# A graph-network kernel's eigensolver: which engine scales the product row and copies the turned column, and who orders GpSimd in the merge levels

## The chip, the cores and the metric

One core of one Trainium2 chip. The time is device microseconds for one launch; all times below are in microseconds (us) unless marked ns. Three runs of the kernel before gave 2366.21, 2367.70 and 2367.98, so the median is 2367.7.

## The reference

`x` has 64 graphs of 256 nodes with 256 features, and `adj` is one 256 x 256 matrix, all fp32. Two layers follow each other:

```python
h = max(layernorm(x), 0)                       # layer 0
x = x + S(S'(S'(h, W1), W2), W3)               # S(h, W) = (adj*adj) @ (h @ W), S' = relu(S)
h = max(layernorm(x), 0)                       # layer 1
deg = A.sum(0) + A.sum(1) - diag(A)            # A = adj
L = rsqrt(deg)[:, None] * (diag(deg) - A) * rsqrt(deg)[None, :]
U = eigh(L).eigenvectors                       # 256 x 256
x = x + U @ (relu((U.T @ h) @ W1' + b1) @ W2' + b2)
```

Layer 0 and the first product of layer 1 (`h @ W1'`) need nothing of the eigenvectors; the rest of layer 1 needs `U`.

## The kernel before

Two kinds of work share the core. The **eigensolver** (class `Eigen`) is one long dependent chain, most of it on VectorE (DVE): it forms L, brings it to tridiagonal form with 254 Householder steps (`tridiagonalize`), solves 16 x 16 leaves (`leaves`), and merges them in four levels of blocks of 32, 64, 128 and 256 (`level`, called from `join`). **Layer 0** (class `Layers`) is TensorE (PE) work on 32 pairs of graphs, with ScalarE (ACT) emptying PSUM banks, GpSimd (POOL) doing the small norm arithmetic and issuing accumulating DMAs. After the eigenvectors are there, layer 1 runs.

**What sets the order.** While the eigensolver is written down, the class `Pace` keeps a model clock for each engine. An eigensolver instruction goes through `Pace.chain`: it works out when its inputs are ready, adds 0.4 on PE or 0.1 on ACT, lets `run` issue layer-0 instructions ("streams") that start before that limit, and then issues its own. A matmul that would pass the limit may be cut at 128 columns (`Op.cut`). The clock uses prices from `Op.__init__`; those of the chain are raised by 6% (`SLOWER = 1.06`). Inside `manual_schedule(engines={PE, Activation})` the program order that results is the order on PE and ACT. The orders on DVE and POOL are left to the framework's scheduler, which works by its own estimate of times. `Pace.fits` decides whether a stream's instruction may go ahead of the limit: with a margin for PE and ACT, and for other engines whenever it starts before the limit.

**A Householder step** on column k (`lo = k + 1`), in the names of the code; a slice `r` has 256 - lo columns, so rows shrink from 255 to 2; up to lo = 127 both halves of 128 rows are live ("first half", 127 steps), afterwards one ("second half", 127 steps):

- `xa`: product of the matrix `a` with the row `xr`, one DVE instruction for each live half, and `ac`, a column.
- `as_row` turns a column into a row: a PE transpose for each live half into PSUM. `pu` (tile psB) is the turned `ac`, `pr` (psA) the turned column `rc = a[:, :, lo]`. The two are issued one after the other, `pu` first.
- scalars: `den`, `gam = 1/den`, `gg = gam*gam`, `gu = gg*u1`, the last two on POOL in the first half and on DVE in the second (`aside`).
- `uau` = sum of `pu * xr`; `gr = pu * gam`, a row, copied out of PSUM with the scale in it; `both = gr*u1 - pr`; `f`; the next row `xn = xr*f - both`; `c`; `wr = xr*c - gr`.
- the update of `a`: two row instructions for each live half, with `wr`, `xr` and the columns `uc`, `wc`.

In the profile a tile has the name of its buffer: `gams` is z, `us` is q, `nbs` is m, `a` is A, the rows r0 and r1 (`junk`, `both`) are r, and `xn` is xr. All kernel lines show as L208, the one place that issues a recorded operation, so the views are read by tile.

**In a level** POOL does three kinds of eigensolver instructions, all `pow` (for `rdq`, `zh`, `rn`). Between them stand layer 0's: three for each norm (`v`, `scale`, `shift`) and three accumulating DMAs for each pair.

Of the kernel before, what the change touches and what calls it, by code (L numbers as in the profile page):

```python
# [23 lines left out]
OP = mybir.AluOpType  # L24
# [14 lines left out]
LEVELS = [32, 64, 128, 256]  # L39
# [120 lines left out]
class Pace:  # L160
# [9 lines left out]
    LEAD = 1.5  # L170

    def __init__(self, nc):
        self.slower, self.lead, self.no_haste = self.SLOWER, 0.0, False
        self.now = Proxy(nc, self.chain)
        self.later = Proxy(nc, lambda op: op)
        self.clock = dict.fromkeys(ENGINES.values(), 0.0)
        self.written, self.read, self.streams, self.on = {}, {}, [], True
# [39 lines left out]
        return self.issue(op, self.slower)  # L217

    def fits(self, op, start, limit, engine):
        if engine is None or op.engine not in ("PE", "ACT"):  # L220
            return start < limit
        if engine == "PE":
            return start < limit + self.HOP * (op.engine == "ACT")
        return start + op.busy + self.lead * (op.engine == "ACT") < limit
# [55 lines left out]
class Eigen:  # L280
# [47 lines left out]
    def row(self, tag):  # L328
        return self.mp.tile([P, N], F32, tag=tag, name=tag)
# [113 lines left out]
    def tridiagonalize(self, a):  # L443
# [6 lines left out]
        nc = self.nc  # L450
# [7 lines left out]
        def as_row(tag, column, halves):  # L458
            ps = self.psum(tag)
            for h in halves:  # L460
                nc.tensor.transpose(
                    ps[:, h * P : (h + 1) * P],
                    column[:, h : h + 1].to_broadcast([P, P]),
                    ident[:, 0, 0:P],
                )
            return ps

        row = lambda tag: self.sp.tile([P, N], F32, tag=tag, name=tag)
# [5 lines left out]
        aside = lambda lo: nc.gpsimd if lo < P else nc.vector  # L474

        def below(xr, lo):

            rest = slice(lo + 1, N)
            sq, tail, alpha = self.row("junk"), *(t[:, lo - 1 : lo] for t in (tails, alphas))
            if lo < P:  # L480
                nc.scalar.activation(sq[:, rest], xr[:, rest], AF.Square, accum_out=tail)
            else:
                self.stt(sq[:, rest], xr[:, rest], 1.0, xr[:, rest], OP.mult, OP.mult, accum=tail)
            nc.gpsimd.tensor_copy(alpha, xr[:, lo : lo + 1])
            return alpha, tail

        def length(xr, lo, tail):

            nn, s0, q, qn = (self.col(c, 1) for c in ("nn", "s0", "q", "qn"))
            x1 = xr[:, lo : lo + 1]  # L490
            self.stt(nn, x1, x1, tail, OP.mult, OP.add)
            if lo < P:
                self.power(s0, nn, 0.5)
                nc.gpsimd.tensor_scalar(q, x1, 0.0, 0.5, OP.is_ge, OP.subtract)
                return nn, s0, q, None
            nc.scalar.activation(s0, nn, AF.Sqrt, bias=guard)
            self.ts(q, x1, 0.0, OP.is_ge, 0.5, OP.subtract)
            self.tt(qn, q, nn, OP.mult)
            return nn, s0, q, qn

        xc = self.col("xc")
        self.tt(xc, a[:, :, 0], self.lower[:, :, 0], OP.mult)
        xr = row("xr")
# [3 lines left out]
        for k in range(N - 2):  # L507
            lo = k + 1
            r, rest = slice(lo, N), slice(lo + 1, N)
            halves = [0, 1] if lo < P else [1]  # L510
            hs = slice(halves[0], H)
            rc = a[:, :, lo]

            nb = nbs[:, k : k + 1]
            if qn is not None:
                rs, qs = self.col("rs", 1), self.col("qs", 1)
                self.recip(rs, s0)
                self.tt(qs, q, s0, OP.mult)
            xa, junk = self.col("xa"), self.row("r0")
            for h in halves:  # L520
                self.stt(junk[:, r], a[:, h, r], 1.0, xr[:, r], OP.mult, OP.mult, accum=xa[:, h : h + 1])
                if h == halves[0] and qn is not None:
                    self.stt(nb, rs, qn, qs, OP.mult, OP.add)
            if qn is None:
                self.stt(nb, q, 2.0, s0, OP.mult, OP.mult)

            ac, uc = self.col("ac"), us[:, :, k]
            self.stt(ac[:, hs], rc[:, hs], nb, xa[:, hs], OP.mult, OP.add)
            pu, pr = as_row("psB", ac, halves), as_row("psA", rc, halves)

            none = self.col("none", 1)
            nc.gpsimd.tensor_scalar(none, tail, 1e-30, 1e30, OP.is_le, OP.mult)
            nc.gpsimd.tensor_tensor(none, none, nn, OP.add)
            den, gg, gu = (self.col(c, 1) for c in ("den", "gg", "gu"))
            gam = gams[:, k : k + 1]
            u1 = xr[:, lo : lo + 1]
            self.tt(u1, u1, nb, OP.add)
            self.stt(den, alpha, nb, none, OP.mult, OP.add)
            self.recip(gam, den)
            self.stt(uc, ident[:, :, lo], nb, xc, OP.mult, OP.add)  # L540
            aside(lo).tensor_tensor(gg, gam, gam, OP.mult)
            aside(lo).tensor_tensor(gu, gg, u1, OP.mult)
            gc, gr = self.col("gc"), row("gr")
            if halves[0]:
                self.tt(gc[:, hs], ac[:, hs], gam, OP.mult)
            else:
                self.ts(gc, ac, gam, OP.mult)

            uau, c = self.col("uau", 1), self.col("c", 1)
            self.stt(junk[:, r], pu[:, r], 1.0, xr[:, r], OP.mult, OP.mult, accum=uau)  # L550
            self.ts(gr[:, r], pu[:, r], gam, OP.mult)

            xn, xcn, both, f = row("xr"), self.col("xc"), self.row("r1"), self.col("f", 1)
            self.stt(both[:, rest], gr[:, rest], u1, pr[:, rest], OP.mult, OP.subtract)
            self.stt(f, uau, gu, gr[:, lo : lo + 1], OP.mult, OP.subtract)
            self.stt(xn[:, rest], xr[:, rest], f, both[:, rest], OP.mult, OP.subtract)
            more = lo + 1 < N - 1
            if more:
                alpha1, tail1 = below(xn, lo + 1)
            self.stt(c, uau, 0.5, gg, OP.mult, OP.mult)  # L560
            wr, wc = row("wr"), self.col("wc")
            self.stt(wr[:, r], xr[:, r], c, gr[:, r], OP.mult, OP.subtract)
            self.stt(wc[:, hs], uc[:, hs], c, gc[:, hs], OP.mult, OP.subtract)
            if more and halves[0]:
                following = length(xn, lo + 1, tail1)
            if halves[0]:
                nc.gpsimd.memset(xcn[:, 0:1], 0.0)
            self.stt(xcn[:, hs], gc[:, hs], u1, rc[:, hs], OP.mult, OP.subtract)
            self.stt(xcn[:, hs], uc[:, hs], f, xcn[:, hs], OP.mult, OP.subtract)
            aside(lo).tensor_tensor(xcn[:, hs], xcn[:, hs], self.lower[:, hs, lo], OP.mult)  # L570
            if more and not halves[0]:
                following = length(xn, lo + 1, tail1)

            for h in halves:
                self.stt(a[:, h, r], wr[:, r], uc[:, h : h + 1], a[:, h, r], OP.mult, OP.add)
                self.stt(a[:, h, r], xr[:, r], wc[:, h : h + 1], a[:, h, r], OP.mult, OP.add)
            xr, xc = xn, xcn
            if more:
                alpha, tail, (nn, s0, q, qn) = alpha1, tail1, following
# [9 lines left out]
        dc = self.col("dnew")  # L589
# [1155 lines left out]
    def join(self, u, ut, bad, reflections=None):  # L1745
        d = self.row("DV")
        self.nc.vector.tensor_copy(d, self.d)
        self.pace.slower, self.pace.lead = self.pace.IN_BLOCKS, self.pace.LEAD
        if reflections is not None:
            reflections = Stream(self.reflections(*reflections))  # L1750
            self.pace.streams = reflections, *self.pace.streams
        zt, dc = self.leaves(d, self.e, bad)
        if reflections is not None:
            self.pace.complete(reflections)
        self.pace.slower, self.pace.lead = self.pace.SLOWER, 0.0
        for n in LEVELS:
            dc = self.level(n, zt, dc, self.rho, self.sg, bad)
        z = self.mat("m0")
        self.copy_out(z, self.transpose(zt))
        self.product(u, self.qt, z)  # L1760
        self.product(ut, z, self.qt)
# [631 lines left out]
```

## Time and profile before

| what | value |
|---|---|
| median of 3 runs | 2367.7 |
| the profiled execution's own time | 2369.36 |
| its span, first to last instruction | 2367.6 |
| TensorE clock granted over the span | 0.994 |
| tridiagonal steps (tile gr) | 25 to 1299 |
| leaves (tile chain from 1324) | to about 1665 |
| levels (matmul psB for zt at 1679, flag at 2173.8) | 1680 to 2173 |
| layer 1 on U (`bank<-hw,u`) | 2181 to 2363 |

The profile has busy times by engine, a picture of 40 slices, groups of instructions by tile, waits (who waited for whom), and a timeline. In a timeline row the first number is the start, the second the duration of the group from its first start to its last end, and what stands in brackets is the engine's idle time before it with the instruction that ended it. Durations on DVE overlap: an instruction that reads 215 ns can be followed by the next start after 120 ns, so the difference of two starts is what an instruction costs its engine. An fp32 matmul of 256 columns is recorded as two instructions.

### The profile page before, as it was taken

The page shows a single profiled execution, that of the slowest core. Times are in us where ns is not written, and L with a number is a line of the kernel's source. Part 1 is how long each engine was busy: PE and PEld are TensorE (multiplying, and loading weights), DVE is VectorE, ACT ScalarE, POOL GpSimd, SP SyncE. Part 2 cuts the span into 40 slices and gives each one's busy share as a digit, 9 for nine tenths or more (in the row PEclk, how much of TensorE's full clock was granted, in tenths as well). Part 3 has the DMA queues.
Part 4 walks back from the last instruction along what each step waited for, and adds up shares of the span by engine and source line. Part 5 has one row for each costly group of instructions (what it writes and reads, how often), then busy time and mean ns, then how long its engine had stood idle before and what let it go on. Part 6 is the DMA issues. An engine that isn't in the chain of part 4 may idle for free. (4 is left out here: it accounts for less than half of the span.)

```text
span 2367.6 us, 40804 instructions
## 1 busy us (share of the span) xinstructions
PE 2290.2 (97%) x10652; PEld 1854.7 (78%) x10652; DVE 2005.0 (85%) x12072; ACT 1183.8 (50%) x2951; POOL 698.7 (30%) x1946
## 2 busy tenths in 40 slices
PE   7999999999999999999999899999999999999999
PEld 4687878787777877787888788777778777887888
DVE  7999999999999999999999899999877687882343
ACT  4455554555555555555555345555554455543322
POOL 3444544445554222222222001111111111111443
PEclk9999999999999999999999999999999999999999
DMA  4022222122222222222222222322322222223675
GB/s 134 23 70 61 65 57 70 51 69 63 59 59 62 72 56 61 69 67 59 72 63 60 58 63 72 72 72 59 72 63 63 59 58 72 54 63 103 217 251 203
DMA packets 91359, 183.26 MB, mean 77 GB/s; under 512 B 8432, under 2 KB 61808, under 8 KB 91120
## 3 DMA queue, kind: packets, MB, share of 16 engines
q0 software_dynamic: 13392, 73.14, 15.6%
q1 hardware_dynamic: 77728, 107.45, 13.4%
q8 instruction: 86, 1.41, 0.2%
q14 instruction: 153, 1.25, 0.2%
HBM read 65.48 MB, written 41.94 MB: 45 GB/s over the span
## 5 line engine op out<-in xcount | busy, mean ns | idle before, releaser
L208 PE MATMUL bank<-forms,L_gnn_W 128*128 128x256 f32 (+2 forms) x2102 | 490.7, 382 | 9.2 <-DVE x L208 6.1
L208 PE MATMUL bank<-L_gnn_W,s 128*128 128x256 f32 x2086 | 476.0, 378 | 4.8 <-ACT s L208 4.7
L208 PEld LDWEIGHTS bank<-forms,L_gnn_W 128*128 128x128 f32 x2102 | 390.6, 191 | 73.3 <-issue 11.7
L208 PEld LDWEIGHTS bank<-L_gnn_W,s 128*128 128x128 f32 x2086 | 391.7, 192 | 57.3 <-ACT s L208 5.7
L208 ACT ACTIVATE s<-bank 128x512 f32<-128x512 f32 (+1 forms) x485 | 278.7, 579 | 174.3 <-PE bank L208 173.3
L208 PE MATMUL bank<-forms,sums 128*128 128x256 f32 (+1 forms) x1512 | 347.0, 377 | 0.0
L208 PEld LDWEIGHTS bank<-forms,sums 128*128 128x128 f32 x1512 | 283.3, 191 | 53.4 <-issue 15.5
L208 PE MATMUL bank<-gt,s 128*128 128x256 f32 (+1 forms) x1036 | 246.3, 377 | 1.1 <-ACT s L208 1.1
L208 PE MATMUL bank<-L_gnn_W,y 128*128 128x512 f32 (+3 forms) x538 | 230.8, 572 | 1.1 <-ACT y L208 1.1
L208 ACT ACTIVATE forms<-bank 128x512 f32<-128x512 f32 x217 | 128.9, 594 | 180.9 <-PE bank L208 180.7
L208 PEld LDWEIGHTS bank<-gt,s 128*128 128x128 f32 x1036 | 188.9, 190 | 24.8 <-ACT s L208 2.6
L208 POOL COPY m<-xr 128x1 f32<-128x1 f32 x254 | 59.9, 236 | 418.1 <-DVE xr L208 418.0
L208 PEld LDWEIGHTS bank<-L_gnn_W,y 128*128 128x128 f32 x538 | 98.7, 190 | 98.2 <-issue 87.3
L208 ACT ACTIVATE junk<-xr 128x254 f32<-128x254 f32 (+63 forms) x127 | 46.0, 362 | 200.5 <-DVE xr L208 200.4
L208 ACT ACTIVATE junk<-x 128x256 f32<-128x256 f32 x256 | 105.8, 413 | 71.9 <-issue 44.0
L208 DVE SCALAR_TENSOR_TENSOR A<-xr,wc,A 128x255 f32<-128x255 f32 (+63 forms) x381 | 139.2, 368 | 0.0
L208 DVE SCALAR_TENSOR_TENSOR A<-wr,q,A 128x255 f32<-128x255 f32 (+63 forms) x381 | 138.0, 365 | 0.0
L208 ACT ACTIVATE junk<-x,nm 128x256 f32<-128x256 f32 x256 | 128.7, 503 | 4.0
L208 PE MATMUL bank<-p,gt 128*128 128x512 f32 (+2 forms) x272 | 122.8, 567 | 0.0
L208 PE MATMUL bank<-gt,h 128*128 128x256 f32 (+1 forms) x520 | 119.1, 379 | 0.1
L208 DVE SCALAR_TENSOR_TENSOR r<-A,xr 128x255 f32<-128x255 f32 (+63 forms) x381 | 117.8, 309 | 0.2
L208 PE MATMUL psB<-ident,ac 128*128 128x128 f32 x381 | 84.7, 277 | 27.2 <-DVE z L208 15.0
(614 smaller groups left out, 4639.5 us busy)
## 6 DMA issues: line engine op xcount, KB each, us to landing
x<-in_x_dram SPq DMA_DIRECT2D x128, 256.0 KB, 3.0
x<-x SPq DMA_DIRECT2D x64, 512.0 KB, 3.5
forms<-forms POOLq DMA_DIRECT2D x31, 768.0 KB, 5.8
s<-s POOLq DMA_DIRECT2D x31, 768.0 KB, 5.9
s<-forms POOLq DMA_DIRECT2D x31, 768.0 KB, 5.8
hw<-hw SPq DMA_DIRECT2D x64, 256.0 KB, 3.1
out_dram<-out SPq DMA_DIRECT2D x64, 256.0 KB, 2.2
L_gnn_W<-in_L_gnn_W_dram SPq DMA_DIRECT2D x1, 2048.0 KB, 11.2
```

The costliest lines, as they stand in the source:

```text
L208: return op.call(*op.args, **op.kwargs)
```

## The change

In the Householder step the scale by `gam` leaves the row and goes to columns and scalars: `gr` is gone, its readers take `pu` out of PSUM; the column `ug = uc*gam` is new, `gu` is now `gam*u1`, `hg = gam*0.5` (POOL in every step) replaces `gg`, and `f` takes two instructions. The transpose of `rc` goes from behind that of `ac` to the start of the step, and ACT copies its result from PSUM into an SBUF row `pr`. In the levels, POOL joins PE and ACT in the program order that `Pace` makes, and a stream's POOL instruction goes ahead of an eigensolver's POOL instruction only if it ends before that one's limit.

```diff
     def fits(self, op, start, limit, engine):
+        if self.pool_too and engine == "POOL" == op.engine:
+            return start + op.busy < limit
         if engine is None or op.engine not in ("PE", "ACT"):
             return start < limit
...
             rc = a[:, :, lo]
+            turned, pr = as_row("psA", rc, halves), row("pr")
+            nc.scalar.copy(pr[:, rest], turned[:, rest])
...
-            pu, pr = as_row("psB", ac, halves), as_row("psA", rc, halves)
+            pu = as_row("psB", ac, halves)
...
-            den, gg, gu = (self.col(c, 1) for c in ("den", "gg", "gu"))
+            den, hg, gu = (self.col(c, 1) for c in ("den", "hg", "gu"))
...
-            aside(lo).tensor_tensor(gg, gam, gam, OP.mult)
-            aside(lo).tensor_tensor(gu, gg, u1, OP.mult)
-            gc, gr = self.col("gc"), row("gr")
+            aside(lo).tensor_tensor(gu, gam, u1, OP.mult)
+            nc.gpsimd.tensor_scalar(hg, gam, 0.5, None, OP.mult)
+            gc, ug = self.col("gc"), self.col("ug")
...
+            self.ts(ug, uc, gam, OP.mult)
...
             self.stt(junk[:, r], pu[:, r], 1.0, xr[:, r], OP.mult, OP.mult, accum=uau)
-            self.ts(gr[:, r], pu[:, r], gam, OP.mult)
...
-            self.stt(both[:, rest], gr[:, rest], u1, pr[:, rest], OP.mult, OP.subtract)
-            self.stt(f, uau, gu, gr[:, lo : lo + 1], OP.mult, OP.subtract)
+            self.stt(both[:, rest], pu[:, rest], gu, pr[:, rest], OP.mult, OP.subtract)
+            self.stt(t, uau, gu, pu[:, lo : lo + 1], OP.mult, OP.subtract)
+            self.tt(f, t, gam, OP.mult)
             self.stt(xn[:, rest], xr[:, rest], f, both[:, rest], OP.mult, OP.subtract)
...
-            self.stt(c, uau, 0.5, gg, OP.mult, OP.mult)
+            self.tt(c, uau, hg, OP.mult)
             wr, wc = row("wr"), self.col("wc")
-            self.stt(wr[:, r], xr[:, r], c, gr[:, r], OP.mult, OP.subtract)
-            self.stt(wc[:, hs], uc[:, hs], c, gc[:, hs], OP.mult, OP.subtract)
+            self.stt(wr[:, r], xr[:, r], c, pu[:, r], OP.mult, OP.subtract)
+            self.stt(wc[:, hs], ug[:, hs], c, gc[:, hs], OP.mult, OP.subtract)
...
-            self.stt(xcn[:, hs], gc[:, hs], u1, rc[:, hs], OP.mult, OP.subtract)
+            self.stt(xcn[:, hs], ac[:, hs], gu, rc[:, hs], OP.mult, OP.subtract)
...
             for h in halves:
-                self.stt(a[:, h, r], wr[:, r], uc[:, h : h + 1], a[:, h, r], OP.mult, OP.add)
+                self.stt(a[:, h, r], wr[:, r], ug[:, h : h + 1], a[:, h, r], OP.mult, OP.add)
...
         self.pace.slower, self.pace.lead = self.pace.SLOWER, 0.0
-        for n in LEVELS:
-            dc = self.level(n, zt, dc, self.rho, self.sg, bad)
+        self.pace.pool_too = True
+        with self.tc.manual_schedule(engines={mybir.EngineType.Pool}):
+            for n in LEVELS:
+                dc = self.level(n, zt, dc, self.rho, self.sg, bad)
+        self.pace.pool_too = False
```

## The prediction

> **What bounds the kernel now.** I read the busy times and the picture first, then the windows by stage, then PE's waits, then the timeline around the long ones.
>
> ```profile
> PE 2290.2 (97%) x10652; PEld 1854.7 (78%) x10652; DVE 2005.0 (85%) x12072; ACT 1183.8 (50%) x2951; POOL 698.7 (30%) x1946
> ...
> PE   7999999999999999999999899999999999999999
> ...
> DVE  7999999999999999999999899999877687882343
> ```
>
> PE is full in nearly every slice, also after the solver ends; DVE, which carries the solver, is full only up to the levels. The same by stage (first the window and its length, then busy PE, PEld, DVE, ACT, POOL):
>
> ```profile
> 56.00:1318.00 1262.00, 1237.64 (x5948) 999.99 (x5947) 1186.03 (x7454) 679.43 (x1745) 495.37 (x1646) 1.00 0.26 62
> 1318.00:1680.00 362.00, 351.52 (x1588) 284.30 (x1587) 336.99 (x2647) 182.90 (x474) 37.36 (x81) 1.00 0.26 63
> 1680.00:2173.00 493.00, 476.03 (x2145) 386.90 (x2145) 371.49 (x1678) 247.27 (x570) 63.91 (x96) 0.98 0.26 63
> 2173.00:2368.00 195.00, 186.48 (x850) 160.70 (x849) 69.03 (x103) 48.50 (x90) 81.10 (x67) 0.98 0.65 222
> ```
>
> PE is idle 24.4 in the tridiagonal steps, 10.5 in the leaves, 17.0 in the levels, 8.5 after the flag. When the solver ends, layer 0 is nearly, not quite, used up: fourth products of the last pair (`L_gnn_W,s`) still run from 2173 to 2185, and its last rows at 2202. So a shorter solver only moves layer-0 matmuls from beside it to behind it. **The time changes by PE's idle time and PE's slow clock, not by DVE's busy time.** PE's waits name the places:
>
> ```profile
> PE psB L208 <- DVE z L208: 15.0, 19, 1.9
> PE psB L208 <- DVE xr L208: 10.6, 12, 1.7
> PE bank L208 <- ACT s L208: 8.6, 6, 3.8
> ...
> PE bank L208 <- DVE x L208: 6.1, 5, 3.6
> PE psA L208 <- DVE m L208: 4.8, 1, 4.8
> ```
>
> The first two are `pu`'s transposes: 26 us in 31 waits over the steps, some 0.8 each. Those steps hold 36 DVE adds of layer 0 (`x<-x,bank`, 0.68 each) that DVE's own order puts among the solver's instructions, as many as there are waits; PE comes to the transpose on time and DVE is late by one add. (z and xr come one to three instructions after `ac`, which is what psB really needs.) The long waits cost twice:
>
> ```profile
> 1763.96 1.89 PE L208 MATMUL bank<-gt,s 128*128 128x256 f32 x8
> 1769.61 6.55 PE L208 MATMUL bank<-L_gnn_W,s 128*128 128x256 f32 x16 [3.76 <-ACT s L208]
> ...
> 1764.14 0.72 POOL L208 TENSOR_TENSOR rdq<-rdq,half 128x2 f32<-128x2 f32 x1 [4.36 <-DVE rdq L208]
> 1764.94 0.19 POOL L208 TENSOR_SCALAR v<-v 128x4 f32<-128x4 f32 x1
> ...
> 2158.35 3.78 PE L208 MATMUL psA<-q,m 128*128 128x256 f32 x8 [4.82 <-DVE m L208]
> ...
> 2168.43 1.89 PE L208 MATMUL psA<-m,QT 128*128 128x256 f32 x8
> ```
>
> Sixteen such matmuls take 3.62 elsewhere and 6.55 after the wait at 1769; eight take 3.78 against 1.89. The windows of 10 us from 1770, 1880 and 2160 show a granted clock of 0.73, 0.77 and 0.78. A wait of 3.6 to 4.8 so costs about 3 more.
>
> **Part 1, the scale to columns.** By differences of DVE starts near 403 (row of 194) and 1000 (row of 76): `gr` goes (0.33; 0.21), in the second half also `gg` (0.07); `c` becomes a plain product (0.12 to 0.07). `ug` comes: a 128x2 instruction costs 0.12 (`uc`) to 0.29 (`gc`, whose reader follows at once); `f` needs one more, 0.07. A first-half step saves 0.20 to 0.03, a second-half one 0.21 + 0.07 + 0.05 - 0.07 - (0.12 to 0.29), so 0.14 to a loss of 0.03. Over 127 steps of each kind: 43 to 0. I take 30, as `ug` stands among independent instructions, like `uc`. It also stands where DVE waits for psB now (22.3 in 74 waits), so part of that wait is filled. All of it lies beside PE's work: the solver ends about 30 earlier, and that alone is worth 0 to the sum. `gu`, until now needed by `f`, is needed by `both`, one row earlier; POOL does it in 0.20 while `gc`, `ug` and `uau` run, and today's wait for `gg` is 0.2 in all. If layer 0's `pow` of 1.04 stands ahead of it, DVE loses up to 1 us in some of 65 places; beside PE again.
>
> What it does to PE goes through the clock of `Pace`. That charges a scalar product 0.126, where the trace shows 0.07; `gr` out at 0.35, `ug` and the second half of `f` in at 0.13 each, so its first-half step shrinks by 0.08 and the real one by up to 0.20. PE is given about 0.1 more work a step than DVE needs, and a late DVE is caught up in fewer steps. Bounds: the 24 stay, or all go. I take a quarter off: **-6**.
>
> One rule speaks against leaving the product in PSUM. Row first: `both` with a PSUM input takes 347 ns (`r<-gr,xr,psA`), `xn` from SBUF alone 345 (`xr<-xr,f,r`), `wr` 346. The Trainium skill, "VectorE: DVE Perf Modes", section "Rules for kernel authors", advises to copy PSUM to SBUF first where many operations follow, and its table in "The TRN2 errata" gives 120 fixed cycles against 58. By the page `wr`, the one row that newly reads PSUM, would lose an estimated 65 ns a step, 16 us of DVE; by the rows nothing. DVE is not the bound, so neither moves the sum.
>
> **Part 2, `rc` turned at the start, copied by ACT.** 254 ACT instructions come: 0.28 for 128x128 out of PSUM, 0.37 for 128x256, so about 75 us in an engine that is busy 679 of 1262; PE waits for no ACT row in the steps from 56 to 1318, so I cost them at nothing. The copy waits in ACT's queue for the transpose; behind it are bank emptyings, with four banks. Were that cover gone, each copy could hold ACT some 0.3. The two transposes keep their 0.11 each. But each step has a second meeting of PE with DVE (in the first half a third: `rc`'s halves become ready at different times). For 254 meetings the trace shows about 90 cuts: `forms,L_gnn_W` needs 31 pairs x 32 matmuls x 2 = 1984 instructions and has 2102, `sums` 1512 for 1488, `s` 2086 for 2048; that is 59, 12 and 19. Two 128-column pieces cost 0.23 twice against 0.43 whole, 0.03 a cut. With 380 more meetings, 0 to 380 cuts, by the same share 135: **+4**. What waits they add: bounded by a rival below, 0 to 38, taken as 0, since a PE that has just waited at psA is on time at psB.
>
> **Part 3, POOL by the clock.** At 1764 the norm's inputs had been ready since 1762.3; `v` stood behind `rdq`, which DVE released at 1764.1. So `shift` came 2 us late, ACT's four `h` instructions waited 2.65 for it, `s` behind them in ACT's queue, and PE 3.76. With `Pace` placing POOL's instructions that one goes first: 3.8 + 2.9 slow clock, **-7**. But a `pow` of the solver then waits behind a norm's three (1.4) or a DMA issue (0.9) more often, beside PE; and everything after is shuffled: the stage shows four long PE waits in 493 us, two of them layer 0's own (the other, 4.6 on `DVE x` near 1872 plus 3 slow, lies in DVE's order and stays). Half a new one: **+3**. Bounds: -14 (both go) to +14.
>
> **Part 4, what the earlier end does.** At 2153 PE has nothing but the last pair left, which waits for its DMA, so 4.8 idle and 3.2 slow follow; near 2192 the last norm costs 2.8 + 0.5 and 1.1 slow. With 30 us of layer 0 left over, the first has cover and the second partly falls beside layer 1's matmuls: **-8 and -2**. If the solver ends less than about 10 earlier, both stay.
>
> **Sum:** -6 + 4 - 7 + 3 - 8 - 2 = -16 on the profiled 2369.4 (span 2367.6 and 1.8 around it), 2353.4. That execution stands 1.7 above the median, so 2352.
>
> **Rivals.**
> *Much better, 2340:* PE is so late throughout that DVE's late adds never reach it: 18 more of the 24 go, and some in the leaves, -12 in all beyond the forecast. For: DVE already waits for psB in 74 steps. Against: 31 PE waits exist beside them.
> *Nothing moves, 2364:* the program is PE's work, the clocked POOL order gives one wait and makes another, the end keeps its last-pair gaps: only the -6 and +4 of the steps remain, and perhaps a wait saved. For: 2290 of 2368 is matmul. It is also the case in which POOL's order comes out as it was.
> *Slower, 2378:* PE comes too early to `rc`. Near 406, DVE runs `xa` of the first half (0.28) before the last update of `a` (406.39), though the program, and so `Pace`, has them the other way; PE's transposes now come 0.1 to 0.4 after `ac` is ready. A margin of 0.3 is gone, and PE could stand up to 0.3 in each of 127 steps. Price 127 x 0.25 = 32, less 12 of psB's waits that it replaces, and the -6 is lost: 2352 + 26. It decides from 0.13 a step on (16 us). Against: in the second half one half is live and the order is the program's, and PE has the more slack the more `Pace` overcharges.
>
> **Numbers.** Forecast 2352 (2345 to 2361) 0.48; much better 0.14; nothing moves 0.22; slower 0.16. The measurement can tell about 0.2% (4.7 us) from no change. Of "nothing moves" I put 0.05 below 2363, 0.14 within, 0.03 above. Faster 0.48 + 0.14 + 0.05 = 0.67, same 0.14, slower 0.19. The range reaches to 2338 and to 2376, leaving out the far ends of the outer cases, under 0.2.
>
> **What would show it.** Right: tridiagonal steps shorter by some 30, PE's idle there near 20 and now partly at psA, the flag near 2140, no PE wait over 3 in the last 60 us before it, and a clock over 0.994. Wrong: PE's waits for psA in the steps above 25 us; new PE waits for ACT rows there; a `pow` of the solver that PE ends up waiting for in the levels; or a solver that does not end earlier.

## The result, and the profile after

Five runs of the changed kernel gave a median of 2392.1 (2390.3 to 2395.3), five of the kernel before 2367.4 (2364.7 to 2368.0): by the medians it is **24.7 slower**, and the ratio on record is 1.0111 times the time before, interval 1.0100 to 1.0123. The forecast was 2352, its range 2338 to 2376. The profiled execution took 2391.75 with a span of 2390.0. All lines of the changed kernel show as L209.

The head of the page (engine, busy time, share of the span, instructions) and three groups (last columns: busy, mean ns of one, idle time before them and what ended most of it):

```profile
PE 2298.2 (96%) x10936; PEld 1854.1 (78%) x10936; DVE 1966.2 (82%) x12199; ACT 1246.8 (52%) x3205; POOL 725.4 (30%) x2073
...
L209 PE MATMUL psA<-ident,A 128*128 128x128 f32 x381 | 107.4, 283 | 45.1 <-DVE A L209 34.7
...
L209 DVE SCALAR_TENSOR_TENSOR r<-psB,xr 128x255 f32<-128x255 f32 (+63 forms) x254 | 73.4, 289 | 69.5 <-PE psB L209 66.0
L209 ACT COPY pr<-psA 128x254 f32<-128x254 f32 (+63 forms) x254 | 66.7, 263 | 119.6 <-PE psA L209 118.5
```

The same stages by windows (window, length, then busy PE, PEld, DVE, ACT, POOL, granted clock):

```profile
56.00:1318.00 1262.00, 1210.99 (x6014) 971.44 (x6013) 1145.59 (x7560) 711.24 (x1929) 516.02 (x1761) 1.00 0.24 59
1318.00:1680.00 362.00, 347.28 (x1563) 278.81 (x1562) 336.44 (x2652) 184.36 (x478) 39.01 (x83) 1.00 0.27 65
1680.00:2173.00 493.00, 486.67 (x2230) 395.79 (x2229) 373.74 (x1684) 257.48 (x593) 70.10 (x100) 1.00 0.28 72
2173.00:2390.00 217.00, 212.78 (x992) 184.14 (x990) 68.13 (x99) 65.97 (x130) 79.29 (x68) 1.00 0.60 192
```

PE's idle time in the four stretches was 24.4, 10.5, 17.0 and 8.5 and is now 51.0, 14.7, 6.3 and 4.2: 15.8 more in all. Its busy time grew by 8.0. Together that is 23.8, against 22.4 that the span grew (the first 56 us are left out of the idle time). So the loss lies in the tridiagonal steps, 26.6 more idle, and the levels and the end give back 15. DVE's busy time in the steps fell by 40, from 1186.0 to 1145.6, yet the steps end where they did: the leaves begin at 1325.2 (1323.7 before). What DVE saved became waiting, as its waits below show.

PE's and DVE's waits over the whole span (waiting engine and its tile, releaser; us, times, longest):

```profile
PE psA L209 <- DVE A L209: 34.7, 42, 2.7
PE psA L209 <- DVE qs L209: 8.5, 11, 1.4
...
PE bank L209 <- ACT s L209: 4.4, 6, 1.4
PE psB L209 <- DVE z L209: 4.4, 9, 0.9
PE psB L209 <- DVE xr L209: 4.3, 9, 1.4
```

```profile
DVE r L209 <- PE psB L209: 66.0, 141, 2.7
```

At psB PE waits 8.7 where it waited 25.6; at psA, where it did not wait in the steps, it waits 43.2. DVE's wait for psB has grown from 22.6 to 66.0. One such place in the timeline:

```profile
153.58 0.46 DVE L209 SCALAR_TENSOR_TENSOR A<-xr,wc,A 128x235 f32<-128x235 f32 x1
...
154.18 0.29 PE L209 MATMUL psA<-ident,A 128*128 128x128 f32 x1 [1.66 <-DVE A L209]
154.18 1.19 PEld L209 LDWEIGHTS bank<-gt,s 128*128 128x128 f32 x6
154.31 1.25 PE L209 MATMUL bank<-gt,s 128*128 128x256 f32 x6
154.32 0.40 DVE L209 SCALAR_TENSOR_TENSOR r<-A,xr 128x234 f32<-128x234 f32 x1
...
154.65 0.46 DVE L209 SCALAR_TENSOR_TENSOR A<-xr,wc,A 128x235 f32<-128x235 f32 x1
...
155.40 0.27 PE L209 MATMUL psA<-ident,A 128*128 128x128 f32 x1
...
155.72 0.36 ACT L209 COPY pr<-psA 128x233 f32<-128x233 f32 x1
```

PE stands 1.66 us before the transpose of the first half of `rc`, until the update of that half (begun 153.58) is written. Layer 0's matmuls on `gt,s` stood behind it in PE's queue and follow at once, with no wait of their own. Then DVE runs `xa` of the first half (154.32) before the last update (154.65), so the second half of `rc` is turned 1.2 us after the first.

**The idle column shows too little.** A matmul followed by another reads longer than it costs: the group `psA<-m,QT` of 8 starts from 2147.4 to 2148.9, some 214 ns apart, and each reads 379. The last matmul before a wait so shows some 165 ns of its tail as busy time. The Trainium skill, "TensorE: Matmul & The Clock Gate", section "Single matmul latency", gives 166 ns as the constant part of a single warm bf16 matmul. The rows here differ by the same amount, but the profile models the ends of matmuls, so they show how the rows are to be read and do not measure the tail itself. So I took the starts instead: for each transpose into psA or psB from 56 to 1318, its start less the shown end of the matmul before it, plus 0.168 for the tail, summed over all that are under 2 us (two transposes that the timeline shows in one row count once). These **gaps** are 32.7 before and 62.5 after, 29.8 more. Three longer ones in the changed kernel (7.4 together) and one before (2.0) are not in them.

### The profile page after: what moved, and what is told of

Same layout as the page of the kernel before. It is cut to its first block, busy times and chain, and to the rows that moved or that the text cites. A ratio compares the mean times of both kernels' runs of the same rounds, so it can differ in the third digit from the quotient of the medians.

```text
span 2390.0 us, 41755 instructions
## 1 busy us (share of the span) xinstructions
PE 2298.2 (96%) x10936; PEld 1854.1 (78%) x10936; DVE 1966.2 (82%) x12199; ACT 1246.8 (52%) x3205; POOL 725.4 (30%) x2073
## 5 line engine op out<-in xcount | busy, mean ns | idle before, releaser
L209 PE MATMUL bank<-forms,L_gnn_W 128*128 128x256 f32 (+2 forms) x2166 | 498.4, 375 | 5.3 <-DVE x L209 3.0
L209 PE MATMUL bank<-L_gnn_W,s 128*128 128x256 f32 (+1 forms) x2168 | 482.4, 371 | 5.0 <-ACT s L209 4.2
L209 PEld LDWEIGHTS bank<-forms,L_gnn_W 128*128 128x128 f32 x2166 | 392.1, 191 | 65.9 <-issue 9.2
L209 PEld LDWEIGHTS bank<-L_gnn_W,s 128*128 128x128 f32 x2168 | 395.8, 192 | 57.3 <-ACT s L209 7.3
L209 ACT ACTIVATE s<-bank 128x512 f32<-128x512 f32 (+1 forms) x485 | 279.8, 582 | 179.7 <-PE bank L209 178.1
L209 PE MATMUL bank<-forms,sums 128*128 128x256 f32 (+1 forms) x1572 | 351.9, 368 | 0.0
L209 PEld LDWEIGHTS bank<-forms,sums 128*128 128x128 f32 x1572 | 286.8, 190 | 55.2 <-issue 17.8
L209 PE MATMUL bank<-gt,s 128*128 128x256 f32 (+1 forms) x1068 | 248.9, 371 | 0.3 <-ACT s L209 0.3
L209 PE MATMUL bank<-L_gnn_W,y 128*128 128x512 f32 (+3 forms) x572 | 235.9, 548 | 1.1 <-ACT y L209 1.1
L209 ACT ACTIVATE forms<-bank 128x512 f32<-128x512 f32 x217 | 129.0, 595 | 178.0 <-PE bank L209 177.4
L209 PEld LDWEIGHTS bank<-gt,s 128*128 128x128 f32 x1068 | 191.9, 191 | 23.1 <-ACT s L209 1.1
L209 POOL COPY m<-xr 128x1 f32<-128x1 f32 x254 | 63.2, 249 | 396.4 <-DVE xr L209 396.1
L209 PEld LDWEIGHTS bank<-L_gnn_W,y 128*128 128x128 f32 x572 | 101.9, 191 | 89.4 <-issue 79.3
L209 PE MATMUL psA<-ident,A 128*128 128x128 f32 x381 | 107.4, 283 | 45.1 <-DVE A L209 34.7
L209 DVE SCALAR_TENSOR_TENSOR A<-xr,wc,A 128x255 f32<-128x255 f32 (+63 forms) x381 | 139.7, 369 | 0.0
L209 DVE SCALAR_TENSOR_TENSOR A<-wr,ug,A 128x255 f32<-128x255 f32 (+63 forms) x381 | 138.5, 365 | 0.0
L209 ACT ACTIVATE junk<-x 128x256 f32<-128x256 f32 x256 | 106.0, 414 | 54.0 <-issue 37.9
L209 ACT ACTIVATE junk<-x,nm 128x256 f32<-128x256 f32 x256 | 129.2, 505 | 3.9
L209 DVE SCALAR_TENSOR_TENSOR r<-psB,xr 128x255 f32<-128x255 f32 (+63 forms) x254 | 73.4, 289 | 69.5 <-PE psB L209 66.0
L209 ACT COPY pr<-psA 128x254 f32<-128x254 f32 (+63 forms) x254 | 66.7, 263 | 119.6 <-PE psA L209 118.5
L209 PEld LDWEIGHTS psA<-ident,A 128*128 128x128 f32 x381 | 51.9, 136 | 96.6 <-ACT s L209 27.2
L209 PE MATMUL bank<-p,gt 128*128 128x512 f32 (+3 forms) x276 | 123.7, 562 | 0.0
```

What stands on the lines that cost most here:

```text
L209: return op.call(*op.args, **op.kwargs)
```

## The experiments

Three theories, all about why PE is late in the steps. *Meeting:* each step now has a second place (in the first half a third) at which the in-order PE must meet DVE, and the 0.4 that the model clock adds there is not enough for DVE to be done; time added beyond it is called **slack** below. (Some expectations call this theory "too early".) *Order:* only DVE's `xa` ahead of the last update, which the model does not know, is to blame. *Copy:* ACT's new row or the new arithmetic is. "Steps end" is the first `chain` instruction of the leaves. Gains and losses in the text are medians less the median of before beside them.

| kernel | median | before beside it | ratio [interval] | gaps at psA, psB | steps end |
|---|---|---|---|---|---|
| before | 2367.4 | | | 32.7 | 1323.7 |
| after | 2392.1 | 2367.4 | 1.0111 [1.0100, 1.0123] | 62.5 | 1325.2 |
| only_move | 2395.0 | 2367.6 | 1.0114 [1.0097, 1.0131] | 59.6 | 1344.0 |
| copy_only | 2428.1 | 2364.9 | 1.0270 [1.0253, 1.0287] | 78.6 | 1349.8 |
| no_pool | 2408.8 | 2367.6 | 1.0174 [1.0157, 1.0191] | 64.4 | 1325.8 |
| only_pool | 2354.5 | 2367.6 | 0.9945 [0.9929, 0.9962] | 33.5 | 1323.5 |
| merged (+0) | 2377.7 | 2366.6 | 1.0050 [1.0033, 1.0067] | 46.7 | 1308.8 |
| slack2 (+0.2) | 2369.3 | 2364.9 | 1.0021 [1.0011, 1.0031] | 39.8 | 1314.4 |
| slack (+0.4) | 2362.7 | 2365.9 | 0.9985 [0.9975, 0.9994] | 32.3 | 1316.5 |
| slack8 (+0.8) | 2382.8 | 2366.6 | 1.0070 [1.0054, 1.0087] | 32.7 | 1361.3 |
| copy_slack | 2380.2 | 2366.6 | 1.0062 [1.0045, 1.0078] | 42.5 | 1334.7 |
| told | 2372.9 | 2365.9 | 1.0030 [1.0020, 1.0040] | 52.1 | 1309.4 |
| dve_order | 2533.9 | 2365.9 | 1.0706 [1.0688, 1.0723] | 157.7 | 1470.5 |
| joint | 2374.7 | 2367.6 | 1.0031 [1.0019, 1.0043] | 22.5 | 1353.8 |
| joint2 | 2355.9 | 2365.9 | 0.9958 [0.9944, 0.9972] | 35.1 | 1323.7 |
| joint2_copy | 2365.6 | 2366.6 | 0.9996 [0.9986, 1.0006] | 33.4 | 1344.2 |
| pool_steps | 2393.1 | 2366.6 | 1.0112 [1.0095, 1.0129] | 58.5 | 1363.6 |
| joint2_pool | 2380.5 | 2366.6 | 1.0064 [1.0047, 1.0080] | 51.5 | 1345.6 |

The gaps end at 1318, so where the steps go on longer, in dve_order above all, they are those of a part of them.

### One part alone

**only_move:** the kernel before, with `rc` turned at the step's start; DVE reads psA itself, there is no copy, and the arithmetic is the old one.

```diff
             rc = a[:, :, lo]
+            pr = as_row("psA", rc, halves)
...
-            pu, pr = as_row("psB", ac, halves), as_row("psA", rc, halves)
+            pu = as_row("psB", ac, halves)
```

> The kernel before with one edit: the transposes of rc stand at the start of the step; DVE reads psA itself as before, gr and POOL's order are unchanged. Theory 'meeting' (PE now meets DVE at rc as well as at ac, too early): PE waits at psA of 30 to 45 us in the steps, psB's waits fall from 26 to under 10, DVE's waits for psB rise from 22 to 50 or more, time 2380 to 2400. Rival 'ACT copy' (the loss comes from ACT standing for psA, which it does for 118 us after the change, and from late bank emptying): without the copy the time stays at 2363 to 2372. Rival 'POOL order' (the loss comes from the clocked POOL order): also 2363 to 2372.

It is 27.4 slower, as much as the whole change and a little more, and its gaps grow by 26.9. PE's waits in the steps (56 to 1318):

```profile
PE psA L208 <- DVE A L208: 20.5, 39, 1.9
PE psA L208 <- DVE qs L208: 11.0, 13, 1.7
PE psB L208 <- DVE z L208: 5.8, 15, 0.8
```

So neither the copy nor the arithmetic is needed for the loss: the move alone makes it.

**only_pool** is the kernel before with the diff of `fits` and `level` alone, **no_pool** the changed kernel without it.

> The kernel before with part 3 alone: POOL in the program order in the levels. 'Meeting' and 'ACT copy' both expect a gain or nothing: PE's idle time in the levels falls from 17 towards 6 to 10 us, time 2355 to 2366. Rival 'POOL order': 2380 or more, with new PE waits in the levels.

> The changed kernel without part 3. 'Meeting' and 'ACT copy': the steps are as in the changed kernel (PE idle about 51 us there), and the levels lose what part 3 gave, so 2392 to 2405. Rival 'POOL order': back to 2360 to 2370.

POOL's order gains 13.0 alone, a little more than expected, and 16.5 within the change (41.2 less 24.7; no_pool lies 3.8 above its range). PE's longest waits from 1680 to the end, before and in only_pool:

```profile
PE bank L208 <- ACT s L208: 7.5, 3, 3.8
PE psA L208 <- DVE m L208: 4.8, 1, 4.8
PE bank L208 <- DVE x L208: 4.6, 2, 3.6
```

```profile
PE bank L209 <- ACT s L209: 5.4, 3, 2.8
PE psA L209 <- DVE m L209: 4.8, 1, 4.8
PE psC L209 <- DVE zc L209: 1.3, 1, 1.3
```

PE's wait of 3.8 at 1769 is 1.7 in only_pool, and the sixteen matmuls behind it take 3.72 where they took 6.55. The two waits for `x` near 1872, 4.6 together, are gone, and the granted clock from 1870 to 1910 is 1.00 where it was 0.91. In the levels PE's idle time falls from 17.0 to 10.9 and the clock rises from 0.98 to 1.00; over the whole span the same 10652 matmul instructions take 7.6 less. The solver changes too, and reaches the flag at 2160.5 instead of 2173.8, though PE's wait of 4.8 for its `m` stays. DVE's waits in the levels (1665 to 2176), before and in only_pool:

```profile
DVE m L208 <- PE psB L208: 40.7, 4, 13.1
DVE rb L208 <- POOL rdq L208: 20.7, 24, 1.1
```

```profile
DVE rb L209 <- POOL rdq L209: 46.5, 24, 6.7
...
DVE m L209 <- PE psB L209: 7.0, 4, 3.5
```

Four transposes into psB that DVE waited up to 13.1 us for now come on time, 33.7 less; DVE pays 25.8 of it back as longer waits for `rdq`. I take it that the model's clock, which places PE's transposes, had POOL's work earlier or later than the chip did as long as POOL's order was not its own; the runs show the two waits, not that reason.

**copy_only:** only_move, and ACT copies the turned column; the arithmetic is still the old one.

```diff
-            pr = as_row("psA", rc, halves)
+            turned, pr = as_row("psA", rc, halves), row("pr")
+            nc.scalar.copy(pr[:, rest], turned[:, rest])
```

> The run only_move (rc turned at the start of the step, old arithmetic with gr, old POOL order; 27 us slower than before) with ACT's copy of the turned column into an SBUF row added, which DVE then reads in place of psA. Between only_move and no_pool (41 us slower) lie the copy and the scale to columns. If the copy costs the 14 us between them: 2403 to 2412, with PE waits for ACT rows that only_move lacks. If the columns do: 2391 to 2400.

The copy costs another 36 (63.3 above the kernel before, only_move 27.4), more than either expectation had. No wait for `pr` explains it; the gaps at the two transposes grow from 59.6 to 78.6 and PE's idle time by 24.2 in all (13.5 of it from 56 to 1318, 6.8 in the levels), its busy time by 7.9. So about half of the cost stands at the meetings. I take it to come through the order that `Pace` writes around one more ACT row a step; no run shows that, and which ACT instruction delays what is not settled. With no_pool (41.2 above) the loss of 24.7 is now split by parts, in this order: **move +27, copy +36, columns -22, POOL's order -16.5.**

### Earlier or later, and both halves at once

**merged, slack2, slack, slack8:** the changed kernel, in which the model takes `rc` for ready only 0.46 after both halves are written, plus 0, 0.2, 0.4 or 0.8. Layer-0 work is then put ahead of the transposes; the data that they wait for are the same.

```diff
-            turned, pr = as_row("psA", rc, halves), row("pr")
+            pace, pr = self.pace, row("pr")
+            pace.floor = max(w[2] for w in pace.written[span(rc[:, hs])[0]]) + 0.46 + 0.4
+            turned = as_row("psA", rc, halves)
+            pace.floor = 0.0
...
-        due = self.ready(op) + self.LATER.get(op.engine, 0.0)
+        due = max(self.ready(op) + self.LATER.get(op.engine, 0.0), self.floor)
```

> The changed kernel with the transposes of rc for both halves at one point, due 0.46 after the last update of A in Pace's clock: the delay of 0.4 of the run slack is taken away again, its single point for both halves stays. Theory 'too early' (PE comes to rc before DVE is done; what helped in slack is the delay): PE's waits at psA are 25 to 40 us in the steps, time 2378 to 2392. Rival 'one meeting more' (each meeting costs, by cuts and tails, and slack helped because it has 127 fewer of them): waits as in slack, about 10, time 2360 to 2370.

> As merged (0 added), slack (0.4 added) and slack8 (0.8 added), with 0.2 added to the due time of rc's transposes. 'Too early' has the waits at psA fall steadily with the delay, from 28 to 9 us between 0 and 0.4, while DVE's waits for PE start to stretch the steps only beyond 0.4: so psA's waits 14 to 22 us, time 2363 to 2372, between the two. A time under 2358 would say that 0.4 is already past the best point.

> The changed kernel with the transposes of rc due 0.4 us later in Pace's clock than now (0.86 after the last update of A, both halves at one point); all else as in the changed kernel. Theory 'order' (DVE runs xa of the first half ahead of the last update of A, so A is about 0.3 later than Pace thinks in every first-half step): the 0.4 covers it, PE's waits at psA fall from 43 to under 12 us, time 2365 to 2378. Rival 'late adds' (single late arrivals of 0.7 us and more, from layer 0's adds on DVE and from waits for POOL, are met at one more place in the step): psA's waits fall by 0.4 each, 43 to about 25, time 2375 to 2385.

> As slack, with 0.8 in place of 0.4. 'Too early': PE's waits at psA go below 5 us, but rc's transposes now crowd those of ac and the row of ac comes later, as in joint; DVE's waits for psB rise to 55 or more and the steps end 10 to 30 us later, time 2362 to 2378. 'One meeting more': as slack, 2360 to 2366.

These four speak for *meeting*: the time follows the slack, down to 0.4 and up again at 0.8, though merged lies just under and slack8 above the range of "too early", and slack below those of both its theories. One meeting for the two halves, at the time of the later one, takes 13.6 of the 24.7 away; 0.2 and another 0.2 of slack gain 6.7 and 7.6, and the gaps fall with them, 62.5, 46.7, 39.8, 32.3. Fewer cuts do not make it: slack has 148 matmul instructions less than the changed kernel, 74 cuts, some 2 us by the estimate of 0.03 a cut. In slack PE's waits in the steps are:

```profile
PE psB L209 <- DVE z L209: 10.2, 16, 1.9
PE psA L209 <- DVE A L209: 4.1, 8, 1.2
PE psA L209 <- DVE qs L209: 3.9, 6, 1.4
```

The best of them, slack, is 3.2 under the kernel before, but it has POOL's order in it: only_pool, without the rest of the change, is 13.0 under. At 0.8 the gaps stay at 32.7, but PE is too late for DVE, and the steps end 45 later than in slack. DVE's wait in the steps (56 to 1318):

```profile
DVE r L209 <- PE psB L209: 88.6, 161, 4.5
```

The solver then outlasts layer 0, and at the end PE waits and runs slow. A window of slack8, its granted clock (0.93) being the last number but two:

```profile
2140.00:2350.00 210.00, 189.53 (x850) 162.47 (x849) 89.55 (x236) 56.88 (x109) 80.92 (x71) 0.93 0.60 192
```

**copy_slack** is copy_only with slack's 0.4.

> The run copy_only (63 us slower than before) with 0.4 more for the due time of rc's transposes and one point for both halves, as slack has them. 'Copy is free where the meeting is not too early': waits at psA fall from 40 to under 12 us, time 2372 to 2385 (it lacks the clocked POOL order, worth 13 to 17, so this is slack's 2363 plus that). 'Copy costs, columns give back': 2390 to 2405.

The same remedy takes 49.6 of copy_only's 63.3 away, and the gaps fall from 78.6 to 42.5. Of the move's 27.4 and the copy's 36 together 13.7 are left, so at least 22 of the copy's 36 go with the slack, if the slack takes no more than 27.4 from the move; only_move with the same slack, which would tell, was not run.

### The order on DVE

**told:** the changed kernel, in which the program writes `xa` of the next step's first half where DVE runs it, ahead of the last update.

```diff
...
+                if h == 1 and lo + 1 < P:
+                    early = self.col("xa"), self.row("r0")
+                    self.stt(early[1][:, rest], a[:, 0, rest], 1.0, xn[:, rest], OP.mult, OP.mult, accum=early[0][:, 0:1])
```

**dve_order:** the changed kernel with DVE, too, bound to the program order in `tridiagonalize`.

```diff
-        d, e, *reflections = self.tridiagonalize(self.laplacian())
+        lap = self.laplacian()
+        with self.tc.manual_schedule(engines={mybir.EngineType.DVE}):
+            d, e, *reflections = self.tridiagonalize(lap)
```

> The changed kernel with xa of the next step's first half written ahead of the last update of A, where DVE runs it anyway, so that Pace's clock has the same order as DVE; the same instructions. 'Order': the first-half waits at psA (33 us in 41 waits) fall under 12, time 2365 to 2378. 'Late adds': they stay at 20 or more, time 2380 to 2395.

> The changed kernel with DVE, too, in Pace's program order during the tridiagonal steps: layer 0's adds and the updates of A then stand on DVE where Pace's clock has them. Both 'order' and 'late adds' expect psA's and psB's waits together to fall from 52 us to under 20; if they stay above 35, neither explains them and what is left is POOL (s, none, gu) and the clock's prices. DVE loses the fillers between dependent instructions, up to 0.5 us a step, so the steps may end later and the time is open: 2365 to 2420.

told takes 17.8 of the 24.7 away, but not as *order* had it: the gaps fall by 10 of the 30 that the change added, and PE's waits at psA in the steps are still 23.5 on `A` and 12.2 on `qs` (32.8 and 8.5 in the changed kernel). The rest goes with steps that end 16 earlier, as merged's do. So *order* explains a third of the waits. Their form is not its form either: 40 waits on `A` of 0.8 on average, not 127 of 0.3. The starts, which show short waits too, say the same: of the 254 transposes of `rc` in the first half 190 have a gap under 0.05, 27 a gap over 0.7, and these 27 (the longest three included) hold 34 of the 46 us. dve_order was to make the model true and so to end the waits. They became the largest of all, and the time far exceeds the expected range (PE's waits over the whole span):

```profile
PE psA L209 <- DVE A L209: 66.8, 111, 3.3
PE psA L209 <- DVE qs L209: 62.8, 113, 2.0
```

As I read the model, it lets DVE begin a later instruction while an earlier one waits for its inputs, as the framework's order does by moving it ahead. In program order DVE is later than that, the steps end 145 later, and PE, which comes by the model, stands.

### One late meeting

**joint, joint2, joint2_copy:** both transposes at `ac`, `rc` just ahead, so that a step has one meeting again. joint and joint2 are the changed kernel (0.46 and 0.24 after `ac` is written), joint2_copy is only_pool with the copy and without the columns.

```diff
+            pace.floor = max(w[2] for w in pace.written[span(ac[:, hs])[0]]) + 0.24
+            turned = as_row("psA", rc, halves)
+            pace.floor = 0.0
             pu = as_row("psB", ac, halves)
+            nc.scalar.copy(pr[:, rest], turned[:, rest])
```

> The changed kernel with the transposes of rc due when those of ac are, just ahead of them, and ACT's copy after both: one meeting of PE and DVE in a step, as before the change; columns, copy and POOL's order stay. 'Meeting': PE's waits at psA and psB together are at most 26 us, DVE's waits for psB under 35, the solver ends before 2140, time 2345 to 2365. 'ACT copy': ACT still copies in every step, now with less time before the row is needed, so 2385 to 2400. 'POOL order': about 2390.

> As the run joint (one meeting, rc's transposes just ahead of ac's), but due 0.22 us earlier, so that the transposes of ac fall where they did before the change and not behind those of rc. Reading of joint: its PE waits were small (17 us in the steps) but the row of ac came 0.22 later in each step, the steps lasted 30 us longer, the solver ended at 2190 and layer 0 ran out before it. By that reading: steps end 30 us or more earlier than in joint, PE's idle time in the steps 18 to 26, time 2343 to 2358. Rival (the columns and ACT's copy cost by themselves, whatever the meeting): 2368 or more, as in joint.

> The run joint2 without the scale to columns: old arithmetic with gr, rc's transposes just ahead of ac's, ACT's copy of the turned column, POOL clocked in the levels; so only_pool plus the copy. Theory 'copy is free where PE and DVE meet once' (in copy_only it cost 36 us because it made the early meeting worse): 2353 to 2362, as only_pool (2354.5) and joint2 (2355.9). Rival 'copy costs, columns give back' (the two only cancel in joint2): 2370 to 2392.

PE's waits of joint2 in the steps:

```profile
PE psB L209 <- DVE z L209: 12.1, 20, 1.2
PE psB L209 <- DVE xr L209: 3.9, 8, 0.9
PE psA L209 <- DVE A L209: 3.1, 5, 1.4
```

joint's gaps are the smallest, 22.5, but it misses its range, for its steps are 30 longer and its end is slack8's: 0.93 of the clock from 2140 to 2350. joint2 keeps the steps' length and beats both kernels, 10.0 under before; only_pool is 13.0 under, with intervals that overlap, so these runs show no gain from the rest of the change. joint2_copy lies between the ranges of its two theories and takes that apart: the copy with its late meeting costs 12 here (1.0 under before for 13.0), and the columns give 9 back, with steps that end 20.5 earlier. The columns without the copy were not tried.

### POOL in the steps as well

**pool_steps** and **joint2_pool:** only_pool and joint2, with POOL's order by the clock in `tridiagonalize` too. If POOL's order was good for 13 in the levels, it might end the late DVE in the steps.

```diff
-        d, e, *reflections = self.tridiagonalize(self.laplacian())
+        lap = self.laplacian()
+        self.pace.pool_too = True
+        with self.tc.manual_schedule(engines={mybir.EngineType.Pool}):
+            d, e, *reflections = self.tridiagonalize(lap)
+        self.pace.pool_too = False
```

> The run only_pool (kernel before, POOL clocked in the levels) with POOL clocked in the tridiagonal steps too. Theory 'late POOL' (PE waits because DVE is late, and DVE is late where a pow of the solver stands behind layer 0's norm or a DMA issue on POOL; in the changed kernel 38% of the transposes that follow within 4 us of such a wait are late, 10% of the others without a wait): DVE's waits for s and none fall from 14 us to under 7, PE's waits in the steps from 25 to under 18, time 2340 to 2352. Rival 'POOL is a bystander': PE's waits stay at 22 or more, time 2350 to 2365, or more where a clocked DMA issue holds up s.

> The run joint2 (columns, copy, one meeting, POOL clocked in the levels) with POOL clocked in the steps too. There DVE waits 21 us for POOL s and 5 each for gu and none. 'Late POOL': these fall under 12 together, PE's waits in the steps from 21 to under 15, time 2338 to 2352, and by the columns' shorter DVE work it is at least as fast as pool_steps. 'POOL is a bystander': 2352 to 2366.

They are 40 and 24 slower than without it, which neither theory had. DVE's waits in the steps of pool_steps:

```profile
DVE den L209 <- POOL none L209: 39.1, 52, 2.3
DVE r L209 <- PE psB L209: 27.9, 60, 2.1
```

The first was 3.6 in the kernel before, and POOL's waits took the place that they were to leave: PE's at psB rose to 51.2. In the changed kernel, of the 99 transposes that have a DVE wait for POOL in the 4 us ahead of them 33 have a gap over 0.1, of the 517 others 63. So a transpose is late more often after a late POOL, a third of them against an eighth; that POOL is the cause for these is likely but not shown, and giving its order to the clock does not cure it here. What makes the others late is left open.

## Why the prediction was wrong

**The failed step** is in Part 2: "What waits they add: bounded by a rival below, 0 to 38, taken as 0, since a PE that has just waited at psA is on time at psB." The second half holds: the waits at psB fell by 17, more than the 12 that I set against. But the first half of the sentence says nothing of what PE waits at psA itself, and that is 43. By only_move the move costs 27.4, inside the bounds that I had written down and put aside. The rival "slower" named the place, PE too early at `rc`, and I gave it 0.16, with a mechanism that is a third of the waits: the reversed `xa`, which told puts right. By the series from merged to slack a second meeting costs as long as it has too little slack, and what comes is some fifty waits of 0.8 on average, not 0.25 in each of 127 steps. So its 2378 was too low as well.

**The copy**, which I "cost at nothing", is the second one: +36 where the meeting is early, +12 where it is late. PE waited on no ACT row in the steps, and hardly any such wait came (1.2 in copy_only). What grew was PE's wait for DVE. My reading is that a row that enters the plan moves the points at which PE commits itself. The sum against what was measured:

| step | forecast | measured |
|---|---|---|
| move: cuts 4, waits 0 | +4 | +27.4 |
| ACT's copy | 0 | +35.9 |
| columns (pace effect) | -6 | -22.1 |
| POOL's order | -4 | -16.5 |
| earlier end | -10 | in the others |
| all | -16 | +24.7 |

**The 36 adds.** I read the 31 waits at psB as 36 late layer-0 adds on DVE, since the counts were alike. In the trace of before only 1 of 46 late transposes has such an add in the 4 us ahead of it, in after 7 of 96. Two equal counts were all that I had.

**Part 1** took 30 off DVE; it was 40. That "the solver ends about 30 earlier" did not follow: steps end at 1325.2 for 1323.7, because DVE waited for psB instead, 66.0 for 22.6, and PE's transposes come by the model's clock. The flag does come 21 earlier, at 2152.7, most of it with POOL's order: no_pool's is at 2168.1. What the columns do give is 22 or 9. From joint2_copy to joint2 the first 127 steps become 18.3 shorter, 0.14 a step, the others 1.5. The pace effect had the model's first-half step 0.08 shorter and DVE's own up to 0.20, and priced that at 6, by the 24 us of waits. Which of the two made the steps shorter no run separates. The rule against leaving a row in PSUM is not seen: `wr` has a median of 343 ns with psB and 346 from SBUF over the same 254 lengths.

**Cuts:** 284 more instructions are 142 more cuts for 135 forecast. That was right; the 4 us rest on the price of 0.03 a cut, which no run tests alone.

**Part 3** had the right sign and was sized too small: -7 + 3 against -13.0 alone, and near its bound of -14. I had the wait near 1872 stay, since it "lies in DVE's order"; with POOL's order alone it went, and its slow clock with it, so both of layer 0's long waits shrank or went and no new one as long came. I missed DVE's own waits for psB, 40.7 in four, as well.

**Part 4** came out, and for another reason. The wait of 4.8 near 2153 is gone and the clock is 0.998; but in only_pool, whose solver ends 13 earlier, it stays (`psA` on `m`, 4.8). In the changed kernel PE lost 27 in the steps and so has layer-0 work left to put there.

**What would show it wrong** was named: "PE's waits for psA in the steps above 25 us". They are.

## What to carry to other kernels

Count the places at which an in-order queue with static order must meet another engine; here each one cost when the other was late, and an instruction that may run earlier is no gain unless its place in the queue has slack (here one meeting less and 0.4 us of slack took away more than the change had cost, and 0.8 lost 19 again). An engine's saved time need not shorten a step whose length another engine's plan helps to set: here 40 us of DVE became waiting. A plan that orders several engines should order those whose times it assumes, but only where the order that it makes is better than the one it replaces; try that stage by stage.

## What the runs showed of the hardware

In these profiles the busy time of a waiting PE overstates its work by the tail that the last matmul's row has, some 165 ns for each wait; waits under that are not seen at all in the idle column. In the steps the idle time at psA and psB shown for only_move is 40.7 (before 23.4), 17 more, while the starts show 26.9 and the time 27.4.

Long waits went with a lower granted clock. At the end of slack8 stand waits of 6.6 (`m`, at 2182) and 8.4 us (a DMA of `hw`, at 2207), with shorter ones between them; the clock is 0.59 from 2180 to 2200, 0.68 from 2200 to 2220 and 1.00 again from 2220 on. In the changed kernel's steps 51 us of idle time, in waits of at most 2.7 us, leave the clock at 1.00 in the row of that window. The row hides short dips: from 300 to 310, behind the wait of 2.7, it is 0.83, and from 590 to 600, with one of 2.4, 0.83 too, while from 148 to 160, with the wait of 1.66 shown above, it is 1.00.
